# Identity products in TensorE's waits, and the product stage's buffers in another order, in a two-layer image model on one core

## The chip, the cores and the metric

The kernel runs on one core of a Trainium2 chip. The metric is the device time of one execution in microseconds (us), the median of several runs. The engines are named as in the profile: PE (TensorE, with PEld for its weight loads), DVE (VectorE), ACT (ScalarE), POOL (GpSimd) and SP (SyncE, which here only issues DMAs). SBUF is the on-chip memory that tiles live in, PSUM the one that PE writes its products to; PSUM has 8 banks of 2 KB per partition.

## What is computed

A batch of 16 images, 128 channels, 32x32 pixels (1024 tokens), goes through two layers. Layer 0 has a linear attention and then a spectral filter (a long causal convolution of the tokens with 16 filters, done by FFT in the reference); layer 1 has two 3x3 convolutions and then a mixture of 64 experts. Cut to what matters:

```python
# layer 0, attention: group norm, q/k/v, softmaxes, context, output projection
qkv = jnp.einsum('bcn,oc->bon', xf, w_qkv)
...
q = jax.nn.softmax(q, axis=-2) * SCALE
k = jax.nn.softmax(k, axis=-1)
context = jnp.einsum('bhdc,bhec->bhde', k, v)
out = jnp.einsum('bhde,bhdc->bhec', context, q)
...
# layer 0, spectral part
out = jnp.einsum('btkd,k,kde->bte', U_plus, s, Mpp)
out = out + jnp.einsum('btkd,k,kde->bte', U_minus, s, Mpm)
...
# layer 1, convolutions
out = _conv3x3(x, w1, stride=1)
out = jax.nn.relu(_bn(out, gamma1, beta1, mean1, var1))
out = _conv3x3(out, w2, stride=1)
out = _bn(out, gamma2, beta2, mean2, var2)
return jax.nn.relu(out + residual)
...
# layer 1, experts: each picks its 8 best tokens, pools them, runs two dense layers
h = jax.nn.gelu(jnp.einsum('ebd,edh->ebh', h, weight1), approximate=False)
...
out = jnp.einsum('ebh,eho->ebo', h, weight2)
...
outputs = outputs.at[jnp.arange(Bn)[:, None], flat_idx].add(weighted)
```

Each part is added to its input; everything is float32.

## The kernel before

The program runs through four stages, in this order. Between them it closes its pools of tiles (named regions of SBUF or PSUM) and opens new ones in the same memory.

**Attention** (classes and functions around L344 to L758; pools `aconst`, `setup`, `work`, `spool`, `xpool`, `ppool` in SBUF and `ps` in PSUM). One sample is a list of small steps, each a method of `Attention`; the table `period` (L729) gives for each step how many samples ahead it runs, and the loop over `p` from -6 to 15 (L747) calls all steps of a period in the order of the table. The engines PE, DVE, ACT and POOL keep the program's order. The first periods are sparse, since only the steps far ahead have a sample to work on. `tokens` transposes a sample on PE (L152), `channels` transposes it back (L162), `k` makes the keys (L439), `group` is a product of one column (L390). The entry `filters` advances a generator that prepares the filters' spectrum: its second step multiplies `phi` by `wf` on PE (L644), later ones load and combine the matrices M_phi into `mst` (L670, L675). Near its end each sample passes through the butterflies on POOL (L277 to L299) into `xf`, one tile of 1 MB in chunks of frequencies, and `odd_turns4` stores it into DRAM tensor `vd` by one DMA (L615). `taps_add` stores the sample itself into `xd` (L634). PSUM tiles carry the tag `big` (3 buffers of two banks) or `s` (2 buffers).

**Products** (L762 to L877). The spectrum has 16 chunks of frequencies. For each chunk `generate` makes a matrix `g` of 64 KB per partition on PE from `mst` and `ph` (L790, PSUM tiles `pg`), `collect` copies it to SBUF by DVE and ACT (L801, L803), `begin` loads the samples' spectra `xc` from `vd` in four batches of four samples (L778) and has POOL build `v` from each batch (L781, L782), `multiply` multiplies `v` by `g` on PE (L814) into PSUM tiles `py`. ACT copies `py` to `yt` (L875), `combine` (L842, L843) adds and subtracts its two halves on DVE, `finish` does the last butterflies on POOL, in the last chunk on DVE (L828 to L831), and stores the chunk to `yd` by two DMAs (L835). Chunk c+1 is generated while chunk c is multiplied, so there are two buffers for `g`, each in a pool of its own (`gpl0`, `gpl1`); chunk 0 uses the first, chunk 15 the second. The pools are opened in the order `gpl0`, `gpl1`, `cpl` (with `v`, `ys`, `ye`, `yt`), `xcl` (`xc`), `psg` (8 PSUM banks). `yd` has two parts: the last two chunks are in the second.

**Convolutions and routing** (L889 to L1489). Pools `cconst`, `first`, `xpool2`, `cwork` in SBUF, `cps` in PSUM (tags `big`, `cv`, `s`). A sample again is a list of steps, methods of `Routed`. Here the order is worked out by a small planner, `planned`, from a table of engine, duration, due time and dependences. `load(b)` loads the sample and its spectrum: the first sample and the first parts of `y` of samples 0 and 1 through POOL's queue, all else through SP's. Then SP loads the convolutions' weights `cw` (L1456) and small vectors. `inverse` (L1087) transforms back on PE, `tokens`, `image`, `channels` are transposes, `conv` makes the products of both convolutions (L969), `logits` (L1274) the routing scores of a pair of samples, `turn` (L152) transposes the gates, `pool` (L1321) gathers the chosen tokens, `pooled` (L1334) transposes the result.

**Experts and output** (L1493 to L1601). For each group of four experts: `hidden` (L1500, L1507), gelu on ACT (L1512), `turn` (L1520), `output` (L1531), `collect` (L1542). The weights stream through a ring of 14 buffers, which are reused buffers of the convolution stage. At the end the experts' results are transposed (L1568), combined with `ob` on DVE (L1572), multiplied by the gates (L1590), added to the samples, and stored (L1601).

A pool that is opened over memory of an earlier pool waits, in every first use of its tiles, until the earlier pools in its place are altogether released. A pool opened with `reuse_waits="tile"` waits tile by tile for those earlier tiles that lay in the same place. Before, only the last pool of the output stage does so (L1581).

Of the kernel before, what the change touches and what calls it, by code (L numbers as in the profile page):

```python
# [8 lines left out]
F32 = mybir.dt.float32  # L9
AF = mybir.ActivationFunctionType  # L10
ALU = mybir.AluOpType
# [3 lines left out]
P = 128  # L15
# [17 lines left out]
NCH = 16  # L33
# [36 lines left out]
def metaformer_kernel(ctx: ExitStack, tc: tile.TileContext, io: dict, out: bass.AP):  # L70
# [83 lines left out]
    def transpose_in_classes(pt, src):  # L154

        for q in range(NQ):
            nc.tensor.transpose(pt[:, q, :], src.rearrange("c (s q) -> c q s", q=NQ)[:, q], ident)

    def transpose_out(pt, src):

# [6 lines left out]
    with ExitStack() as l0:  # L167
# [43 lines left out]
        with ExitStack() as a0:  # L211
# [128 lines left out]

            def small(shape, name):
                return work.tile(shape, F32, name=name, tag=name, bufs=5)

            class Attention:  # L344

# [266 lines left out]

                def odd_turns4(self):
                    butterflies(self.ao, self.xf, 1, self.sd)
                    nc.sync.dma_start(  # L615
                        vd[:, :, self.b, :].rearrange("c p w -> p c w"),
                        self.xf.rearrange("p c x r m j -> p c (x r m j)"),
                    )

                def taps(self):  # L620

# [124 lines left out]
            with tc.manual_schedule(engines=PINNED):  # L746
                for p in range(-reach, B):  # L747
                    next(preparing, None)
                    for name, d in period:
                        b = p + d  # L750
                        if name == "filters":
                            next(setting, None)
                        elif 0 <= b < B:
                            if name == "tokens":
                                samples[b] = Attention(b)
                            getattr(samples[b], "q_" if name == "q" else name)()
                assert next(preparing, None) is None
                for _ in setting:  # L758
                    pass


        with ExitStack() as g0:  # L762
            gpl = [g0.enter_context(tc.tile_pool(name=f"gpl{i}", bufs=1)) for i in range(2)]
            cpl = g0.enter_context(tc.tile_pool(name="cpl", bufs=2))
            xcl = g0.enter_context(tc.tile_pool(name="xcl", bufs=1))
            psg = g0.enter_context(tc.tile_pool(name="psg", bufs=8, space=PSUM))
            gs, vs = {}, {}
            NB = EPR // 4

# [69 lines left out]

            def combine(c, m, ys, t):  # L840

                nc.vector.tensor_tensor(ys[:, :, 0, m], t[:, 1], t[:, 0], ALU.add)  # L842
                nc.vector.scalar_tensor_tensor(  # L843
                    ys[:, :, 1, m], t[:, 1], -1.0, t[:, 0], ALU.mult, ALU.add
                )
                if m == NM - 1:
                    finish(c, ys)

            with tc.manual_schedule(engines=PINNED):
# [5 lines left out]
                for c in range(NCH):  # L855
# [4 lines left out]
                    for m in range(NM):  # L860
# [10 lines left out]
                        fresh = set()  # L871
                        for x in range(2):
                            multiply(c, m, x, py, fresh)
                        t = cpl.tile([P, 2, JL // RG, C], F32, name="yt", tag="yt", bufs=1)
                        nc.scalar.copy(t, py)  # L875
                        waiting = c, m, ys, t
                combine(*waiting)  # L877


# [11 lines left out]
    with ExitStack() as c1:  # L891

        cconst = c1.enter_context(tc.tile_pool(name="cconst", bufs=1))
        first = c1.enter_context(tc.tile_pool(name="cfirst", bufs=1))
        xpool = c1.enter_context(tc.tile_pool(name="xpool2", bufs=1))
        work = c1.enter_context(tc.tile_pool(name="cwork", bufs=2))
        cps = c1.enter_context(ExitStack())
        ps = cps.enter_context(tc.tile_pool(name="cps", bufs=2, space=PSUM))

# [73 lines left out]
        def big():  # L975
            return ps.tile([P, N], F32, name="big", tag="big", bufs=2)

        def tokens(t):
            return t.rearrange("p (j c) -> p j c", c=C)

# [2 lines left out]
        def load(b):  # L983
# [3 lines left out]
            (nc.sync if b else nc.gpsimd).dma_start(xt[b], xd[b])  # L987
            yts[b] = first.tile([P, 2, 2 * NM, C], F32, name="y", tag="y", bufs=2)
            for i, js in enumerate((slice(P - 2 * JL), slice(P - 2 * JL, P))):
                (nc.gpsimd if b < 2 and i == 0 else nc.sync).dma_start(  # L990
                    yts[b][js].rearrange("p r x e -> p r (x e)"),
                    yd[i][:, :, b].rearrange("j r x e -> j r (x e)"),
                )
# [458 lines left out]
        with tc.manual_schedule(engines=PINNED | {mybir.EngineType.SP}):  # L1452
# [5 lines left out]
            for j in range(2):  # L1458
                nc.sync.dma_start(b2[j * E : (j + 1) * E, :], w2[:, HID, :])
            samples = [None] * B  # L1460
            for b, name in order:
                if name == "yin":
                    if b > 1:
# [8 lines left out]
                if name == "tokens2":  # L1472
                    if b // 2 in AWAY:
                        nc.sync.dma_start(xd[b], samples[b].x)
                    if b % 2 == 0 and b // 2 - 1 in AWAY:
                        load_half(b // 2 - 1 - AWAY[0])
                if b == B - 1 and name == "inverse":
                    for h in range(5, 9):
                        load_half(h)
# [68 lines left out]
        with tc.manual_schedule(engines=PINNED):  # L1548
# [18 lines left out]
            for q in range(NPAIR):  # L1567
                nc.tensor.transpose(  # L1568
                    pob[:, q, :], ot[:, 2 * q : 2 * q + 2, :].rearrange("p j e -> p (j e)"), ident
                )  # L1570
            for q in range(NPAIR):
                nc.vector.scalar_tensor_tensor(  # L1572
                    ob[:, q], pob[:, q], rs[:, q : q + 1], ob[:, q], ALU.mult, ALU.add
# [183 lines left out]
```

## Time and profile before

| what | us |
|---|---|
| median of 3 runs | 1266.36 |
| the runs | 1265.75, 1269.21, 1266.36 |
| the profiled execution | 1271.15 |
| its span, first to last instruction | 1269.4 |
| mean granted clock of PE | 0.965 |

Busy shares of the span: PE 91%, DVE 74%, ACT 57%, POOL 48%.

| stage | from about | to about |
|---|---|---|
| attention | 0 | 387 |
| products | 387 | 669 |
| convolutions and routing | 681 | 1166 |
| experts | 1166 | 1239 |
| output | 1239 | 1269 |

How to read it: "L814 PE MATMUL py<-g,v 128*32 128x128 f32 x8" is eight matrix instructions of line 814 that write tile `py` from `g` and `v`; a float32 product of the program is two such instructions. In the timeline the first two numbers are start and length in us, and the bracket gives how long the engine stood idle before and what the profile thinks released it. A wait for several things is put down to the one that came last in the record. "SPq" and "POOLq" are queues of an engine on which DMAs are issued; a DMA in the chain of waits is drawn from its issue to its landing. The granted clock is the share of full speed that PE was given.

### The profile page before, as it was taken

The numbers are of one execution on the slowest core, as the hardware profiler recorded it, in microseconds if no ns is written. First come the engines' busy times: TensorE is split into PE (matmuls) and PEld (weight loads), VectorE is DVE, ScalarE is ACT, GpSimd is POOL, SyncE is SP. The second block draws the span as 40 slices with busy tenths as digits, with TensorE's granted clock in tenths as the row PEclk, the third lists the DMA queues.
The fourth block names the chain that finished last, engine by engine and source line by source line (L and its number), as shares of the span: only waits on it lengthen the run. The fifth ranks groups of instructions, "written<-read, shape, count | busy, mean of one in ns | idle before, by whom it ended". The sixth has DMA issues, their size and how long they took to land. (4 is left out here: it accounts for less than half of the span.)

```text
span 1269.4 us, 34066 instructions
## 1 busy us (share of the span) xinstructions
PE 1149.6 (91%) x14244; PEld 934.4 (74%) x14244; DVE 934.9 (74%) x1944; ACT 726.0 (57%) x1420; POOL 603.9 (48%) x801
## 2 busy tenths in 40 slices
PE   4889999999997999999994999999999999986995
PEld 3677777777776988888883888888888888862442
DVE  5788888887774777776764799888898988881235
ACT  4777777767554777777761355555655655543111
POOL 2335545565566688887872434343333433220002
PEclk8999999999998999999997999999999999996998
DMA  7105343443336344444448423233233223245996
GB/s 264 33 30 165 117 138 124 133 158 92 125 118 192 94 137 136 131 133 126 124 137 268 112 51 83 83 98 120 83 100 117 72 95 113 88 147 186 353 378 265
DMA packets 91226, 175.13 MB, mean 138 GB/s; under 512 B 5952, under 2 KB 42048, under 8 KB 90432
## 3 DMA queue, kind: packets, MB, share of 16 engines
q1 hardware_dynamic: 90192, 169.54, 40.8%
q0 software_dynamic: 880, 3.41, 0.8%
q8 instruction: 112, 1.84, 0.6%
q14 instruction: 42, 0.34, 0.1%
HBM read 110.28 MB, written 62.65 MB: 136 GB/s over the span
## 5 line engine op out<-in xcount | busy, mean ns | idle before, releaser
L969 PE MATMUL pcv<-v,cw 128*128 128x256 f32 x1152 | 258.2, 380 | 1.3 <-POOL v L1157 1.3
L969 PEld LDWEIGHTS pcv<-v,cw 128*128 128x128 f32 x1152 | 214.7, 190 | 34.4 <-issue 4.9
L801 DVE COPY g<-pg 128x512 f32<-128x512 f32 x196 | 128.2, 682 | 82.4 <-PE pg L790 82.2
L803 ACT COPY g<-pg 128x512 f32<-128x512 f32 x316 | 161.4, 606 | 32.5 <-PE pg L790 31.6
L790 PE MATMUL pg<-ph,mst 32*128 32x128 f32 x4096 | 140.9, 278 | 7.4 <-issue 5.9
L790 PEld LDWEIGHTS pg<-ph,mst 32*128 32x128 f32 x4096 | 127.2, 187 | 20.7 <-issue 13.9
L814 PE MATMUL py<-g,v 128*32 128x128 f32 x4096 | 128.4, 276 | 10.5 <-POOL v L781 6.0
L814 PEld LDWEIGHTS py<-g,v 128*32 128x32 f32 x4096 | 110.2, 111 | 21.8 <-POOL v L781 6.4
L144 ACT ACTIVATE tok<-tok,sts 128x128 f32<-128x128 f32 x256 | 101.9, 480 | 16.8 <-DVE sts L1044 13.4
L135 DVE BATCH_NORM_STATS2 bst<-big 128x6 f32<-128x256 f32 x256 | 91.0, 416 | 21.5 <-PE big L152 12.4
L781 POOL TENSOR_TENSOR v<-xc 128x256 f32<-128x256 f32 x128 | 100.4, 807 | 9.3 <-DVE g L801 9.3
L626 PE MATMUL big<-u,mu 128*128 128x128 f32 (+4 forms) x384 | 86.0, 380 | 0.0
L1157 POOL TENSOR_TENSOR v<-abss 128x256 f32<-128x256 f32 x64 | 49.0, 786 | 68.1 <-DVE abss L1153 56.7
L277 POOL TENSOR_TENSOR xf<-ab 128x256 f32<-128x256 f32 x34 | 24.7, 727 | 114.0 <-DVE ab L244 113.9
L1176 POOL TENSOR_TENSOR yo<-abss 128x256 f32<-128x256 f32 x32 | 23.5, 734 | 108.9 <-DVE abss L1172 108.9
L626 PEld LDWEIGHTS big<-u,mu 128*128 128x128 f32 x384 | 56.7, 191 | 18.0 <-issue 15.4
L875 ACT COPY yt<-py 128x512 f32<-128x512 f32 x64 | 37.5, 585 | 51.7 <-PE py L814 31.3
L559 PE MATMUL big<-wf,ub 128*128 128x256 f32 x256 | 63.6, 393 | 0.2
L144 ACT ACTIVATE tt<-tt,sts 128x128 f32<-128x128 f32 x128 | 51.1, 481 | 14.6 <-DVE sts L1044 14.6
L1598 POOL TENSOR_TENSOR xb<-yt,xb 128x1024 f32<-128x1024 f32 x3 | 7.1, 2353 | 107.6 <-ACT yt L1597 107.6
L782 POOL TENSOR_SCALAR v<-v 128x256 f32<-128x256 f32 x64 | 55.0, 860 | 5.6
L464 POOL TENSOR_TENSOR ke<-ke,ks 128x1024 f32<-128x1024 f32 x16 | 30.6, 1913 | 55.7 <-DVE qs L472 44.1
(251 smaller groups left out, 2493.7 us busy)
## 6 DMA issues: line engine op xcount, KB each, us to landing
we<-in_weight SPq DMA_DIRECT2D x32, 1024.0 KB, 7.9
vd<-xf SPq DMA_DIRECT2D x16, 1024.0 KB, 5.1
xc<-vd SPq DMA_DIRECT2D x64, 256.0 KB, 3.4
yd<-ys SPq DMA_DIRECT2D x32, 512.0 KB, 3.8
y<-yd SPq DMA_DIRECT2D x14, 896.0 KB, 6.6
x<-in_x SPq DMA_DIRECT2D x16, 512.0 KB, 4.4
mi<-in_M_phi SPq DMA_DIRECT2D x16, 512.0 KB, 4.6
xd<-x SPq DMA_DIRECT2D x16, 512.0 KB, 6.1
```

The costliest lines, as they stand in the source:

```text
L135: nc.vector.bn_stats(bst[:, j : j + 2, :].rearrange("p j s -> p (j s)"), src[:, j : j + 2, :].rearrange("p j c -> p c j"),)
L144: nc.scalar.activation(dst[:, j, :], src[:, j, :], AF.Identity, bias=nm[:, j : j + 1], scale=r[:, j : j + 1],)
L559: nc.tensor.matmul(dst, self.ub[:, q, :], wf[:, q, :], start=True, stop=True)
L626: nc.tensor.matmul(self.pa[:, a:hi], mu[:, NF - 1 - si, tap, :], self.u[:, a - tap : hi - tap], start=(tap == 0), stop=(tap == KU - 1),)
L781: nc.gpsimd.tensor_tensor(vv[:, x, 1:, bs], e, o, op)
L782: nc.gpsimd.tensor_scalar(v[:, :, 0, bs], v[:, :, 2, bs], -1.0, None, ALU.mult)
L790: nc.tensor.matmul(pg[r][:, i], mst[rs, 4 * q + i, :], ph[rs, c, :], start=True, stop=True,)
L801: nc.vector.tensor_copy(dst, src)
L803: nc.scalar.copy(dst, src)
L814: nc.tensor.matmul(py[rows, x, kl, :], v[:, (x * NM + m) * JL + jl, 1 - ri : 3 - ri, :] .rearrange("p k b -> p (k b)"), g[:, ((x * 2 + ri) ...
L969: nc.tensor.matmul(pc[:, i], wt[:, dy, k, :], v[:, k, dy * WT : dy * WT + HT], start=(dy == 0), stop=(dy == 2),)
L1157: nc.gpsimd.tensor_tensor(v[:, k, WT : WT + HT], self.ab[:, 0], self.ab[:, 1], op)
```

## The change

It has these parts.

1. A helper `keep` writes `count` products of the identity with itself (128x256, one product each) into a PSUM tile `wm` that nobody reads. It takes a buffer of tag `s` in attention and of tag `cv` later. It is called in attention after `tokens` of sample 1 (9 products), after the first `filters` entry after the first period (8), after `channels` of sample 0 (3) and `k` of sample 1 (3); at the head of the convolution stage (26); after `turn` (4) and `pooled` (8) of sample 13, `logits` (11) and `turn` (1) of sample 15; and before the last combination with `ob` (4).
2. The store of the last sample's spectrum to `vd` is split: chunk 0 alone, then chunks 1 to 15.
3. In the product stage the pools are opened in the order `gpl0`, `cpl`, `gpl1`, `xcl`, `psg`, and all but `gpl0` wait tile by tile.
4. In the last chunk ACT copies only the first half of `py`, into one of two slots of `yt`, and DVE reads the second half from PSUM.
5. The pools of the convolution stage except `cconst` wait tile by tile.
6. The first part of `y` of sample 1 is loaded through SP's queue, not POOL's.

```diff
+    def keep(ps, tag, count):
+
+        if count:
+            wm = ps.tile([P, 2, P], F32, name="wm", tag=tag, bufs={"s": 2, "cv": 3}[tag])
+        for _ in range(count):
+            nc.tensor.matmul(
+                wm, ident, ident.unsqueeze(1).to_broadcast([P, 2, P]), start=True, stop=True
+            )
...
+            idle = {("tokens", 1): 9, ("filters", 0): 8, ("channels", 0): 3, ("k", 1): 3}
...
-                    nc.sync.dma_start(
-                        vd[:, :, self.b, :].rearrange("c p w -> p c w"),
-                        self.xf.rearrange("p c x r m j -> p c (x r m j)"),
-                    )
+                    for cs in (slice(0, 1), slice(1, NCH)) if self.b + 1 == B else (slice(NCH),):
+                        nc.sync.dma_start(
+                            vd[cs, :, self.b, :].rearrange("c p w -> p c w"),
+                            self.xf[:, cs].rearrange("p c x r m j -> p c (x r m j)"),
+                        )
...
                         if name == "filters":
                             next(setting, None)
+                            keep(ps, "s", idle.pop((name, 0), 0) if p > -reach else 0)
...
                             getattr(samples[b], "q_" if name == "q" else name)()
+                            keep(ps, "s", idle.get((name, b), 0))
...
-            gpl = [g0.enter_context(tc.tile_pool(name=f"gpl{i}", bufs=1)) for i in range(2)]
-            cpl = g0.enter_context(tc.tile_pool(name="cpl", bufs=2))
-            xcl = g0.enter_context(tc.tile_pool(name="xcl", bufs=1))
-            psg = g0.enter_context(tc.tile_pool(name="psg", bufs=8, space=PSUM))
+            gpl = [g0.enter_context(tc.tile_pool(name="gpl0", bufs=1))]
+            cpl = g0.enter_context(tc.tile_pool(name="cpl", bufs=2, reuse_waits="tile"))
+            gpl.append(g0.enter_context(tc.tile_pool(name="gpl1", bufs=1, reuse_waits="tile")))
+            xcl = g0.enter_context(tc.tile_pool(name="xcl", bufs=1, reuse_waits="tile"))
+            psg = g0.enter_context(tc.tile_pool(name="psg", bufs=8, space=PSUM, reuse_waits="tile"))
...
-                nc.vector.tensor_tensor(ys[:, :, 0, m], t[:, 1], t[:, 0], ALU.add)
-                nc.vector.scalar_tensor_tensor(
-                    ys[:, :, 1, m], t[:, 1], -1.0, t[:, 0], ALU.mult, ALU.add
-                )
+                a, b = t
+                nc.vector.tensor_tensor(ys[:, :, 0, m], b, a, ALU.add)
+                nc.vector.scalar_tensor_tensor(ys[:, :, 1, m], b, -1.0, a, ALU.mult, ALU.add)
...
-                        t = cpl.tile([P, 2, JL // RG, C], F32, name="yt", tag="yt", bufs=1)
-                        nc.scalar.copy(t, py)
-                        waiting = c, m, ys, t
+                        if c + 1 < NCH or m == 0:
+                            t = cpl.tile([P, 2, JL // RG, C], F32, name="yt", tag="yt", bufs=1)
+                        if c + 1 < NCH:
+                            nc.scalar.copy(t, py)
+                            waiting = c, m, ys, (t[:, 0], t[:, 1])
+                        else:
+                            nc.scalar.copy(t[:, m % 2], py[:, 0])
+                            waiting = c, m, ys, (t[:, m % 2], py[:, 1])
...
-        first = c1.enter_context(tc.tile_pool(name="cfirst", bufs=1))
-        xpool = c1.enter_context(tc.tile_pool(name="xpool2", bufs=1))
-        work = c1.enter_context(tc.tile_pool(name="cwork", bufs=2))
+        first = c1.enter_context(tc.tile_pool(name="cfirst", bufs=1, reuse_waits="tile"))
+        xpool = c1.enter_context(tc.tile_pool(name="xpool2", bufs=1, reuse_waits="tile"))
+        work = c1.enter_context(tc.tile_pool(name="cwork", bufs=2, reuse_waits="tile"))
...
-        ps = cps.enter_context(tc.tile_pool(name="cps", bufs=2, space=PSUM))
+        ps = cps.enter_context(tc.tile_pool(name="cps", bufs=2, space=PSUM, reuse_waits="tile"))
...
+        idle = {(13, "turn"): 4, (13, "pooled"): 8, (15, "logits"): 11, (15, "turn"): 1}
...
-                (nc.gpsimd if b < 2 and i == 0 else nc.sync).dma_start(
+                (nc.gpsimd if b + i == 0 else nc.sync).dma_start(
...
             samples = [None] * B
+            keep(ps, "cv", 26)
...
+                keep(ps, "cv", idle.get((b, name), 0))
...
+            keep(ps, "cv", 4)
             for q in range(NPAIR):
                 nc.vector.scalar_tensor_tensor(
```

## The prediction

> **What bounds the kernel now.** I read the clock row of the page first, then what PE waited for, then the timeline where the long waits lie, then the chain of waits.
>
> Page, slices of 31.7 us (tenths):
>
> ```profile
> PE   4889999999997999999994999999999999986995
> PEclk8999999999998999999997999999999999996998
> ```
>
> PE is the bound almost everywhere. The slices that miss are the start, slice 12 (attention to products), slice 21 (products to convolutions), and slices 35-36 and 39 (end of the convolutions, output). In four of these five the granted clock is low too.
>
> PE's waits (total, times, longest):
>
> ```profile
> PE big L1087 <- DMA y<-yd: 16.2, 1, 16.2
> ...
> PE big L152 <- DVE rs L1301: 7.1, 7, 5.5
> ...
> PE py L814 <- POOL v L781: 6.0, 1, 6.0
> PE big L644 <- DMA phi<-in_phi: 6.0, 1, 6.0
> ...
> PE pfy L1590 <- DVE ob L1572: 2.3, 1, 2.3
> ```
>
> Each is one event at one of those places, so a change there is worth its own wait plus the slow clock after it.
>
> Busy time in stretches (length, busy PE, PEld, DVE, ACT, POOL, clock, DMA share, GB/s):
>
> ```profile
> 400.00:410.00 10.00, 3.16 (x56) 2.53 (x60) 1.03 (x2) 1.05 (x3) 9.64 (x14) 0.59 0.41 110
> ...
> 670.00:680.00 10.00, 0.00 (x0) 0.00 (x0) 0.00 (x0) 0.00 (x0) 0.00 (x0) 0.50 0.81 266
> 680.00:690.00 10.00, 6.10 (x37) 5.75 (x38) 6.22 (x11) 0.00 (x0) 5.25 (x7) 0.75 0.92 310
> ```
>
> The clock halves after a gap and DMA, not PE, fills 670-690. Timeline of the first boundary:
>
> ```profile
> 388.88 0.37 SPq L615 DMA_DIRECT2D vd<-xf  x1
> ...
> 389.35 4.25 SPq L634 DMA_DIRECT2D xd<-x  x1
> ...
> 398.12 1.42 POOL L781 TENSOR_TENSOR v<-xc 128x256 f32<-128x256 f32 x2 [9.27 <-DVE g L801]
> ...
> 405.87 0.66 PE L814 MATMUL py<-g,v 128*32 128x128 f32 x8 [6.00 <-POOL v L781]
> ```
>
> POOL sits idle 9.27 us; the DVE named was working all along, so the true releaser is another: the store of xd, issued at 389.35, lands 8.5 us later, 397.85. Chain of waits, second boundary and tail:
>
> ```profile
> 669.62 8.89 DMA yd<-ys
> ...
> 686.34 14.09 DMA y<-yd
> ...
> 1148.09 4.77 PE big L1274 x8
> ...
> 1161.43 3.73 PE pp L1321 x32
> 1166.45 1.94 PE ph L1500 x8
> ...
> 1202.99 1.00 PE ph L1500 x8
> ```
>
> The same L1500 group takes 1.94 us early and 1.00 later: the tail runs at half clock until 1180.
>
> **What the skill says.** "TensorE: Matmul & The Clock Gate", Part 1: the clock is judged in free-running windows of 3413 ns, half rate after an idle one. The trace agrees: its clock steps (12.65, 19.45, 26.3, 401.8, 412.0, 668.0, 685.1, 1145.9, 1180.0, 1241.5) lie on a 3.413 us grid within 0.06. On that grid, windows with PE busy up to 0.34 all lost the clock, two of 0.43 kept it, one of 0.44 and one of 0.52 lost it; regaining took a window of 0.92 or more, and some of 0.98 to 1.00 did not do. The same page, Part 4: transposes don't count as busy the same way; the trace has one stretch made of them (1144.9-1148.0) and it lost the clock. "DMA: Bandwidth & Descriptors", Queues, rings and completion order: each ring is consumed in order; the trace agrees, y waits 14.09 us behind 2.3 MB of cw. No page bears on the pools' waits.
>
> **Price of one identity product.** 128x256 f32, two instructions. L969 has the shape: x12 in 2.59 us, 0.216 each, so 0.43 us a call at full clock, 0.86 at half.
>
> **A. Start (keep 9, 8, 3, 3).** PE ends the second token transposes at 10.1 and waits for phi until 16.1. Nine calls fill 10.1-14.0 (their PSUM slot is free at 9.5). The L644 group then took 5.35 us for 16, ending 21.45; warm it is 16 x 0.216 = 3.46: 1.9 less. DVE sat idle 5.12 us on it (through ACT's L235), so this moves everything. Eight calls end at 23.0, before L390 (25.8 - 1.9 = 23.9); then L152 1.73 becomes 1.04 and L162 1.91 becomes 1.07, partly beside ACT. Bounds 0 (a window with 0.4 of activity ends the clock anyway) to 3.4; I take 2.0. The threes lie in waits of 2.0-2.1 us (before 31.48 and 46.97): nothing.
>
> **B. Attention to products.** Summing the tiles in the order of the pools (KiB per partition): attention's work tiles lie at 51-147, xf at 147-163, the x tiles at 163-195. Before, the matrix buffers take 26-154 and v lies at 154 and up, over xf and x, hence the wait for xd's landing. After, the product buffers lie at 90-134, over work tiles only, whose last reader is POOL's L299 at 388.85. So POOL starts when the first xc lands, 387.4 + 3.3 = about 390.7, and does three batches of 2.3 us (1.42 + 0.85) by 397.6. The fourth needs the last sample's vd store; its chunk 0 now goes alone and first, so that xc no longer waits for the whole 1 MB at 396.6 but only for SP to come past xd at 393.6. It queues behind vd and xd, which leave the engines by 396: landed about 397, v whole at 399.9. PE ends its generation of g at 399.87, held by the copies into g (DVE 389.00 to 398.66). The 6.00 and 0.97 us of stalls go, and with them the half clock of 401.8-412.0: the second py group, at 413.26 before, comes one period of 3.88 us after 399.87, at 403.75, 9.5 earlier. The new late one is g's copies, level with v. The second matrix buffer now lies over xf and x and waits for 397.85, but it is first written at about 399.2. psg by tile lets PE begin 1.4 us sooner, but g's copies start at 388.9 all the same: 0.1. If the fourth xc lands 2-3 us later, 6.5 remains. I take 9.0.
>
> **C. Products to convolutions.** Chunk 14 reads the first matrix buffer for the last time near 656.4; xp0 and y0 lie over it alone. By tile, POOL's load of x0 no longer waits for the last product (3.40 us of idle, 666.21) but goes after L831 at 662.8; y0 follows. y1's first part leaves POOL's queue and stands on SP behind y0's second part. The last chunk's half copies take ACT from 0.59 to about 0.35: 0.25. Before the yd store's landing DMA then has 3.5 MB, not 4.4, and 3.4 us more: landed near 673.6, not 678.5. PE's first inverse moves from 681.87 to about 677.5; 26 calls from 665.6 end at 665.6 + 11.2 = 676.8, just before. But SP now has y1's 0.9 MB ahead of cw, x2, y2: 3.3 us at 280 GB/s. y2, which lands at 700.43 and gates DVE's L1016 and so the first conv a, gains only 4.9 - 3.3 = 1.6; the path through sample 0 gains 4.4. Both meet at conv a. I take 2.8; bounds 0 and 4.4. Memsets and the other tiles' waits are hidden by those loads.
>
> **D. Tail (keep 4, 8, 11, 1).** Fours fill the 2.33 us before L1321 (1134.93), which is warm then, 1.97 not 3.06, but DVE's L1232 ends at 1139.25 in any case: 0.2. Eight (3.45) lie in the 4.35 us gap before 1144.92. The transposes there are paced by ACT (8 x 0.38); a window mostly of them may lose the clock all the same. If not, logits end at about 1150.9, not 1152.84: 2.0, taken at half, 1.0. Eleven (4.7) lie in 5.55 us. L152 1.94 to 1.06: 0.9. L1321 3.68 to 1.97: 1.7. From its end, before: L1500 for group 2 ends 15.3 us later (1180.37). After: ACT's L1552 (2.44) and table load (1.28) hold the first gelu until 3.9; then 0.6, L1520 0.75, L1500 and L1507 2.13, L1531 1.08, 0.75, 1.07: 10.2. Gain 5.1. Later groups run at 3.94 us as before: weights queue ahead by over 10 us (14 halves landed by 1148). Sum 0.2 + 1.0 + 0.9 + 1.7 + 5.0 = 8.8; bounds 2 and 10.
>
> **E. Output (keep 4).** 1.7 us in the 2.33 before 1240.88. The first four pairs fall from 3.4 to 1.7; the first store goes 1.6 earlier, and stores of 8 MB near 400 GB/s then set the end: 1.5.
>
> **Sum.** 2.0 + 9.0 + 2.8 + 8.8 + 1.5 = 24.1. PE is the bound between these places, so they add. The profiled execution took 1271.15 (span 1269.4 and 1.75 around): it would be 1247. It lies 4.8 above the median of 1266.36, which is what I forecast from: 1242.
>
> **Rivals.** (1) The calls don't bridge all gaps (windows at 0.4 of activity): A 0, D 3, E 0.5, B and C as above less a little: 14, so 1252. For it: windows of 0.44 and 0.52 that lost the clock. Against: two of 0.43 that kept it, and the calls fill most gaps to 0.8. (2) Everything carries: A 3.4, B 9.5, C 4.4, D 10, E 1.6: 29, so 1237. Against it is y2's place on SP. (3) Slower: the identity products themselves run at half clock, 0.86 a call, and stand before the work they precede. Eight at the start end 2.5 late; 26 end near 685.7, 3.8 after the old first inverse; eight and eleven push L152 to 1163.5, 5.1 late; the last four 1.1. That is 12.5 lost against B's 9.0: 1270. It decides from about 0.76 us a call. Against it: L969 in the same shape holds full clock all through the convolutions. (4) The tile waits do nothing: B stands by the new order of pools alone, C is lost: inside the range.
>
> **Chances.** Forecast 0.53 (own range 1237-1248), (1) 0.22, (2) 0.18, (3) 0.05, (4) 0.02. Leaving out (3) and the outer ends of (1) and (2): 1233 to 1255. About 0.3%, 4 us, is what can be told from no change: faster 0.93, same 0.02, slower 0.05.
>
> **What would show it.** B: POOL's first v near 391, no PE wait at py, clock 1.0 in that slice. C: xp0 issued near 663, inverse near 4 us earlier, y2's landing against it. D: L1274, L1321 and the first L1500 at 2-3, 2.0 and 1.0 us. E: first store 1.5 us sooner after the last transposes. I am wrong if the clock row still falls at these places, or if a keep group ends after the wait it lies in.

## The result, and the profile after

| | before | after |
|---|---|---|
| median | 1266.89 (1266.36 in the first three) | 1252.55 |
| single runs | 1265.75 to 1269.21 | 1249.26 to 1255.48 (4 runs) |
| the profiled execution | 1271.15 | 1249.26 |
| its span | 1269.4 | 1247.5 |
| mean granted clock in it | 0.965 | 0.994 |

The ratio is 0.9884, 95% interval 0.9851 to 0.9917: 14.3 us faster by the medians, 21.9 us between the two profiled executions. The forecast was 24.1 us, to 1242. The time lies inside the outer range given (1233 to 1255), outside the forecast's own (1237 to 1248); the gain is 10 us short of the forecast. The profiled execution of the changed kernel is the shortest of its four, that of the kernel before lies above all its runs shown: the difference between 21.9 and 14.3 is part of the answer.

Line numbers have moved: L644 is now L656, L781 L796, L814 L829, L790 L805, L969 L988, L1274 L1295, L1321 L1342, L1500 L1523, L1590 L1614; the identity products are L164. One identity product is called a call below, as in the prediction. First the two rows of the page, slices of 31.2 us:

```profile
PE   7889999999999999999988899999999999998996
PEclk9999999999999999999999999999999999999998
```

Slice 0 rises from 4 to 7, slice 12 from 7 to 9, slice 36 from 6 to 8. Slices 20 to 22, the second boundary, show 8s where one slice showed 4. The start, in the timeline of before and of after:

```profile
16.10 5.35 PE L644 MATMUL big<-wf,phi 128*128 128x256 f32 x16 [6.00 <-DMA phi<-in_phi]
```

```profile
10.53 4.19 PE L164 MATMUL wm<-ident 128*128 128x256 f32 x18
15.88 3.69 PE L656 MATMUL big<-wf,phi 128*128 128x256 f32 x16 [1.16 <-DMA phi<-in_phi]
```

PE's waits after (total, times, longest):

```profile
PE pg L805 <- issue: 8.2, 16, 1.1
...
PE pcv L988 <- POOL v L1178: 2.7, 1, 2.7
...
PE py L829 <- issue: 2.3, 1, 2.3
...
PE big L152 <- DVE rs L1322: 1.9, 7, 0.6
```

The waits of 16.2, 6.0 and 6.0 us are gone or down to 1.2 us (the first is filled by the identity products, which can't be told from work here), but one ahead of the convolutions' products (before: L969 after POOL's L1157) has grown from 1.3 to 2.7 us, and waits that nothing releases ("issue") have grown from 5.9 + 2.0 to 8.2 + 2.3 us. Timeline of the first boundary:

```profile
385.39 3.95 SPq L646 DMA_DIRECT2D xd<-x  x1
386.80 1.43 POOL L796 TENSOR_TENSOR v<-xc 128x256 f32<-128x256 f32 x2 [2.33 <-PE pg L805]
...
394.77 1.42 POOL L796 TENSOR_TENSOR v<-xc 128x256 f32<-128x256 f32 x2 [0.94 <-DMA xc<-vd]
...
395.56 0.43 PE L829 MATMUL py<-g,v 128*32 128x128 f32 x8 [0.18 <-POOL v L796]
```

POOL begins 1.4 us after SP starts on xd's store, and no longer 8.8 after; PE's first product waits 0.18 us, not 6.00. The chain of waits (start, length), second boundary and tail:

```profile
660.44 5.13 DMA yd<-ys
...
675.28 13.68 DMA y<-yd
693.53 7.09 PE pcv L988 x24
...
1137.92 3.82 PE big L1295 x8
...
1149.45 2.02 PE pp L1342 x32
```

The store of yd takes 5.13 us, not 8.89. The 24 products of L988 take 7.09 us: the records show the clock at half from 693.48 to 696.89, after the wait of 2.72 us ahead of them. The logits took 4.77 and now 3.82, L1342 3.73 and now 2.02.

### The profile page after: what moved, and what is told of

The parts are those of the page before. It is cut to its first block, busy times and chain, and to the rows that moved or that the text cites. A ratio compares the mean times of both kernels' runs of the same rounds, so it can differ in the third digit from the quotient of the medians.

```text
span 1247.5 us, 34359 instructions
## 1 busy us (share of the span) xinstructions
PE 1166.0 (93%) x14398; PEld 952.3 (76%) x14398; DVE 940.9 (75%) x1944; ACT 725.2 (58%) x1420; POOL 603.1 (48%) x800
## 3 DMA queue, kind: packets, MB, share of 16 engines
q1 hardware_dynamic: 90448, 170.46, 41.2%
## 4 chain that ended last, share of the span: by engine, by line
PE 60%; DVE 23%; ACT 7%; DMA 4%; issue 4%; POOL 2%; SPq 0%; POOLq 0%; ACTq 0%; DVEq 0%
PE pg L805 10%; PE pcv L988 10%; PE py L829 10%; PE big L638 6%; DVE bst L135 4%; PE big L152 3%; PE big L171 3%; PE big L570 2%; PE big L450 2%; PE big L533 2%; PE big L432 2%; DMA y<-yd 2%; DVE abss L1231 1%; DVE xp L1253 1%; ACT tt L144 1%
## 5 line engine op out<-in xcount | busy, mean ns | idle before, releaser
L988 PE MATMUL pcv<-v,cw 128*128 128x256 f32 x1152 | 259.9, 382 | 2.7 <-POOL v L1178 2.7
L988 PEld LDWEIGHTS pcv<-v,cw 128*128 128x128 f32 x1152 | 215.9, 191 | 36.3 <-issue 4.9
L805 PE MATMUL pg<-ph,mst 32*128 32x128 f32 x4096 | 144.2, 280 | 9.2 <-issue 8.2
L805 PEld LDWEIGHTS pg<-ph,mst 32*128 32x128 f32 x4096 | 128.7, 186 | 25.7 <-issue 16.7
L829 PE MATMUL py<-g,v 128*32 128x128 f32 x4096 | 125.1, 274 | 4.6 <-issue 2.3
L829 PEld LDWEIGHTS py<-g,v 128*32 128x32 f32 x4096 | 108.2, 110 | 12.7 <-POOL v L797 2.6
L796 POOL TENSOR_TENSOR v<-xc 128x256 f32<-128x256 f32 x128 | 99.0, 797 | 3.3 <-PE pg L805 2.3
L286 POOL TENSOR_TENSOR xf<-ab 128x256 f32<-128x256 f32 x34 | 24.8, 729 | 110.4 <-DVE ab L253 110.3
L144 ACT ACTIVATE tt<-tt,sts 128x128 f32<-128x128 f32 x128 | 51.1, 481 | 14.5 <-DVE sts L1065 14.5
L570 PEld LDWEIGHTS big<-wf,ub 128*128 128x128 f32 x256 | 46.2, 190 | 8.8 <-ACT xn L423 3.0
```

Source lines behind the costliest of these rows:

```text
L144: nc.scalar.activation(dst[:, j, :], src[:, j, :], AF.Identity, bias=nm[:, j : j + 1], scale=r[:, j : j + 1],)
L570: nc.tensor.matmul(dst, self.ub[:, q, :], wf[:, q, :], start=True, stop=True)
L796: nc.gpsimd.tensor_tensor(vv[:, x, 1:, bs], e, o, op)
L805: nc.tensor.matmul(pg[r][:, i], mst[rs, 4 * q + i, :], ph[rs, c, :], start=True, stop=True,)
L829: nc.tensor.matmul(py[rows, x, kl, :], v[:, (x * NM + m) * JL + jl, 1 - ri : 3 - ri, :] .rearrange("p k b -> p (k b)"), g[:, ((x * 2 + ri) ...
L988: nc.tensor.matmul(pc[:, i], wt[:, dy, k, :], v[:, k, dy * WT : dy * WT + HT], start=(dy == 0), stop=(dy == 2),)
```

## Experiments

Each kernel's time stands against runs of the kernel before that were taken beside it on the same chip: the first four experiments on one chip, all others on another. To see where time went, I cut each profile at the same instructions: the end of the last attention product (L626 before), the 65th product instruction of the product stage (the 413.26 of the prediction), the stage's last, the convolutions' 25th, their last, the end of the experts' last transposes (L1568). In us; in brackets PE's idle time over 0.3 us that nothing releases. The convolutions took 422.7 to 423.7 in all and are left out.

| kernel | attention ends | first products | products (unreleased) | to convolution 25 | tail | output | span |
|---|---|---|---|---|---|---|---|
| before | 386.3 | 26.9 | 252.4 (7.8) | 42.1 | 107.5 | 30.8 | 1269.4 |
| after | 382.0 | 18.9 | 255.8 (9.7) | 41.2 | 98.7 | 27.9 | 1247.5 |
| a1_after | 385.2 | 18.5 | 257.7 (12.7) | 43.5 | 99.0 | 27.9 | 1254.9 |
| a2_keeps_only | 382.6 | 26.9 | 255.3 (10.0) | 44.3 | 98.5 | 28.1 | 1259.4 |
| a3_pools_only | 386.5 | 18.8 | 247.7 (4.7) | 45.0 | 101.2 | 30.8 | 1253.2 |
| a4_order_alone | 388.9 | 19.1 | 248.0 (4.2) | 48.3 | 102.2 | 31.5 | 1261.3 |
| b1_shift41 | 388.8 | 20.7 | 249.7 (6.2) | 42.6 | 98.8 | 29.3 | 1253.0 |
| b2_shift9 | 385.2 | 23.2 | 250.3 (5.7) | 41.0 | 98.2 | 28.0 | 1249.0 |
| b3_shift25 | 386.2 | 19.7 | 240.7 (1.3) | 44.4 | 98.9 | 28.0 | 1240.9 |
| b4_y2_first | 382.3 | 20.8 | 253.2 (8.9) | 40.0 | 98.6 | 28.0 | 1245.9 |
| c1_wide64 | 383.8 | 19.6 | 250.2 (7.2) | 41.6 | 100.8 | 28.0 | 1247.1 |
| c2_wide64_y2 | 382.7 | 18.8 | 241.7 (2.4) | 40.4 | 98.8 | 28.0 | 1233.3 |
| c3_y1_on_pool | 382.0 | 19.8 | 255.8 (11.4) | 42.5 | 100.8 | 28.0 | 1251.6 |
| c4_keep_transposes | 384.4 | 19.1 | 259.6 (13.0) | 40.1 | 101.1 | 27.1 | 1254.5 |

### The change in parts

The kernel before, beside these four: 1263.19 (51 runs, all but one between 1257.15 and 1273.49). The profiled 1271.15 lies far up in this spread. Its mean granted clock was 0.965; the middle one of the 50 is 0.9685. The changed kernel once more:

> The changed kernel again, for the spread of its times. Theory P (the median is 14 below before, not 24, because the grid of clock windows falls differently in each execution and a drop or two stays in most of them): times spread over 1248 to 1256, and the mean clock of an execution goes with its time, 0.990 for the long and 0.994 for the short. Theory Q (the first profile was an odd one and the change is worth 14): times within 1251 to 1254, and the profile shows the stage gains to be smaller than in the first one at the same clock.

Measured: 1248.65, ratio 0.9886 (0.9842 to 0.9929). The gain by medians is 14.5 us again; the 21.9 between the first two profiles doesn't hold. Its six runs spread from 1245.11 to 1257.13, and the two longest have the lowest clocks (0.988 and 0.989, the others 0.992 to 0.994): theory P rather than Q.

The identity products alone, with the old pools and loads:

```diff
+                            keep(ps, "s", idle.get((name, b), 0))
...
+            keep(ps, "cv", 26)
...
+                keep(ps, "cv", idle.get((b, name), 0))
...
+            keep(ps, "cv", 4)
```

> The kernel before with the identity products alone: old pools, old order, old queues. If the steps add up: start 2 to 4, nothing at the first boundary (POOL still begins its v near 398 less the start's gain, PE still waits 6 us), nothing at the second, tail near 9, output 1.5 to 3, so 1251 to 1254. Rival (the products hold the clock only where the loads of the new pools also come earlier, or are mostly luck): less than 6 gained, above 1260. In the profile L1321 of the last pair takes 2.0 and L1500 of the first group 1.07 in the first case.

Measured: 1261.35, ratio 0.9977 (0.9961 to 0.9993). The number is the rival's, but the pieces that it doubted are there: attention ends some 4 us sooner (382.0 to 385.2 with calls in the three profiles so far, 386.3 to 388.9 in the three without), the last L1321 takes 1.97 us and not 3.68, the output is some 3 us shorter. The product stage (2.9 us longer than before) and the second boundary (2.2) give 5 us back.

The buffers alone (all but the identity products):

```diff
+        count = 0
         if count:
```

> The changed kernel with no identity product (the counts are 0); pools, split store, queues and half copies stay. If the steps add up: first boundary 8 to 9, second 1 to 3, so 1255 to 1258; the clock still falls at 12.6, near 668 and four times after 1130. Rival (the product stage gives part back to waits for instructions, 3.5 us in the first profile): 1259 to 1261, and the product stage from its second py group to its last is 255 to 256 us long and not 252.4.

Measured: 1257.15, ratio 0.9949 (0.9931 to 0.9968). The number is inside the 1255 to 1258, but not as the sum had it: the first boundary gained 8.1 us as expected, while the second lost 2.9 in the profile where 1 to 3 were to be gained. PE's first inverse comes 13.0 us after the last product there and no longer 16.2, but y of sample 2 lands 36.2 us after it (before: 34.8). Only the new order of the product stage's pools, and the split store, with the old waits:

```diff
-            gpl = [g0.enter_context(tc.tile_pool(name=f"gpl{i}", bufs=1)) for i in range(2)]
+            gpl = [g0.enter_context(tc.tile_pool(name="gpl0", bufs=1))]
             cpl = g0.enter_context(tc.tile_pool(name="cpl", bufs=2))
+            gpl.append(g0.enter_context(tc.tile_pool(name="gpl1", bufs=1)))
...
+                    for cs in (slice(0, 1), slice(1, NCH)) if self.b + 1 == B else (slice(NCH),):
```

> The kernel before with only the new order of the product stage's pools and the split store; every pool still waits for whole pools. Theory O (the place of the buffers is what counts: the work tiles under them are free at 388.9): POOL's first v near 391, PE's wait at py below 2 us, 1257 to 1259. Rival W (the tile waits do it): POOL's first v near 398 as before, the 6 us wait stays, 1265 to 1267.

Measured: 1263.86, ratio 1.0004 (0.9972 to 1.0035). Its timeline at both boundaries:

```profile
392.27 3.74 SPq L635 DMA_DIRECT2D xd<-x  x1
393.33 1.42 POOL L783 TENSOR_TENSOR v<-xc 128x256 f32<-128x256 f32 x2 [1.98 <-ACT g L805]
...
402.61 0.43 PE L816 MATMUL py<-g,v 128*32 128x128 f32 x8 [0.22 <-POOL v L783]
```

```profile
665.18 0.62 POOL L989 DMA_DIRECT2D xp<-xd  x1 [10.70 <-DMA yd<-ys]
...
679.29 2.04 PE L1089 MATMUL big<-wi,y 128*128 128x128 f32 x8 [23.38 <-DMA y<-yd]
```

At the first boundary the order does everything: 26.9 us become 19.1 here and 18.8 with tile waits, and the identity products do nothing there (26.9). At the second it is given back: x and y of sample 0 start on POOL's queue at 665.18, when the last store of yd has landed, 9.3 us after the last product (before: 0.6), and land with SP's loads at 679.20. The wait is 23.38 us instead of 16.2. With tile waits that load starts 3.8 us ahead of the last product (a3), so the tile waits keep part of what the order gains; half copies and the other queue for y of sample 1 also differ between the two kernels and were not taken apart here. Theory O was right about POOL and PE, and its 1257 to 1259 wrong: it had not looked at the second boundary.

The tails of the last two kernels are that of the kernel before, instruction for instruction on PE. Yet they take 101.2 and 102.2 us, not 107.5. The first two groups of L1500, in stretches (length, busy PE, PEld, DVE, ACT, POOL, clock, DMA share, GB/s), of before, of order alone, of buffers alone:

```profile
1166.45:1178.68 12.23, 11.51 (x73) 3.65 (x73) 0.98 (x2) 3.71 (x8) 0.00 (x0) 0.50 0.74 252
```

```profile
1162.98:1170.52 7.54, 6.41 (x72) 2.55 (x72) 0.98 (x2) 3.71 (x8) 0.00 (x0) 1.00 0.85 302
```

```profile
1155.39:1163.08 7.69, 6.41 (x73) 2.55 (x73) 0.98 (x2) 3.85 (x8) 0.00 (x0) 1.00 0.87 296
```

After has 7.69 there as well. In both these kernels, which have no identity products, the clock comes back before this stretch; in the profile of before it stayed at half until 1180. What that stretch gained between the two first profiles, 4.5 us, doesn't need the calls. (With them, two of ten further profiles took 10.4 us there, after a fall of the clock at 1153 and 1158: they don't settle it either.) No second profile of the kernel before shows how often it stays at half so long.

### Instruction blocks in the product stage

In the product stage PE, which is busy almost all the time, stands still now and then, and nothing releases it. Of the changed kernel, timeline:

```profile
507.36 1.61 PE L805 MATMUL pg<-ph,mst 32*128 32x128 f32 x46 [0.88 <-issue]
...
512.18 1.06 PE L805 MATMUL pg<-ph,mst 32*128 32x128 f32 x28 [0.47 <-issue]
```

and the page's rows of DMA queues:

```profile
q8 instruction: 113, 1.85, 0.6%
```

113 packets of 16.4 KB for 28,982 recorded PE instructions: 256 to a packet. Counting PE's recorded instructions from the start, of 163 unreleased waits over 0.35 us (weight loads, product stage of the table, all 14 profiles) 160 fall on number 193 or 194 of a block of 256. In the changed kernel ten of the eleven of PE's over 0.4 us in that stage end 2.2 to 2.4 us after a q8 packet has started. The two above: packets at 505.01 and 509.76, PE goes on at 507.36 and 512.18. So these are waits for instructions. The Trainium skill, "Runtime: NRT & Kernel Launch", section Instruction fetch mechanics, states blocks of 16 KiB, 256 instructions, and calls the crossing "mostly hidden". The block's size agrees; the cost doesn't: here a crossing costs up to 2.3 us, and the waits of the stage add up to 9.7 us.

A chunk of the stage makes 1024 PE instructions, four blocks, so a boundary falls on the same place of the loop in every chunk. The 23 identity products before the stage are 92 instructions and move it. To move it further I put narrow products of the identity at PE's head, 41, 9 and 25 of them in three kernels:

```diff
+            ws = ps.tile([P, 2, P], F32, name="ws", tag="s")
+            for _ in range(41):
+                nc.tensor.matmul(ws[0:32, 0], ident[:, 0:32], ident, start=True, stop=True)
             for n in range(2):
                 pw = ps.tile([P, P], F32, name="pw", tag="s")
```

> The changed kernel with 41 more, narrow products (32 columns of the identity into an unread tile, about 31 ns an instruction pair, some 3 us in all) in TensorE's first wait, from 2.5 to 5.9 us. They add 41 x 4 = 164 PE instructions ahead of the product stage, which with the 92 of the identity products there make 256. Theory F (instruction fetch): in the product stage PE's idle stretches without a releaser all end 2.2 to 2.4 us after the start of a 16 KB packet of the instruction queue, and fall on number 193 or 194 of a block of 256 instructions; the identity products moved the blocks against the loop, from a place that costs 251.5 us (pools alone, order alone) to one that costs 259.5 to 261.3. Back at a whole block the stage takes 250 to 253 us, such waits sum to 5 to 7 us and not 14 to 16, and the time is 0.6% below the changed kernel's: ratio to before about 0.982. Theory R (the waits are chance, or come from the DMA load): stage 258 to 262 us, ratio 0.9886 as before.

> The same with 9 narrow products, 36 instructions, so that the blocks stand half a block (128) from where they stood before the change. F: the stage's length differs from that of the changed kernel (259.5 to 261.3 us) by more than its two profiles differ from each other, in the direction that the place in the loop gives; its level can't be told ahead. R: 258 to 262 us, ratio 0.9886.

> The same with 25 narrow products, 100 instructions, three quarters of a block (192). F and R as for half a block: F wants the stage's length to change with the place, R wants 258 to 262 us in all three.

Measured against 1263.06: 1252.97, ratio 0.991 (0.9888 to 0.9932); 1244.71, 0.9864 (0.9828 to 0.9901); 1242.70, 0.9866 (0.9819 to 0.9914). By the place in the block, with all kernels of the table:

| PE instructions added ahead, modulo 256 | product stage | unreleased |
|---|---|---|
| 0 (before, a3, a4, b1) | 247.7 to 252.4 | 4.2 to 7.8 |
| 92 (after, a1, a2, b4, c3, c4) | 253.2 to 259.6 | 8.9 to 13.0 |
| 128 (b2) | 250.3 | 5.7 |
| 192 (b3, c1, c2) | 240.7 to 250.2 | 1.3 to 7.2 |

The expectations count the stage from the ninth product instruction, 3.4 to 6.4 us more than the table. In that count b1, b2 and b3 took 254.9, 256.7 and 244.3 us: all below theory R's 258 to 262, b1 above F's 250 to 253. The six at 92 lie above all eight others, whatever their pools: theory F holds for that step. Among the other places the spread at one place is too wide to rank them. By the whole time none of the three ratios is told from the changed kernel's 0.9884, since the intervals overlap. My price for the narrow products was wrong. They took 11.93 us for 41:

```profile
2.54 11.93 PE L347 MATMUL ws<-ident 128*32 128x128 f32 x82 [2.54 <-POOL ident masks.py:199]
```

That is 0.145 us for a matrix instruction with its weight load where I had taken 31 ns, attention ended at 388.8, and b1's total missed its 0.982.

Next, the same shift without that cost: 64 columns and twice the calls where the change has 256.

```diff
-                wm, ident, ident.unsqueeze(1).to_broadcast([P, 2, P]), start=True, stop=True
+                wm if tag == "cv" else wm[:, 0, 0:64],
+                ident,
+                ident.unsqueeze(1).to_broadcast([P, 2, P]) if tag == "cv" else ident[:, 0:64],
+                start=True, stop=True,
...
-            idle = {("tokens", 1): 9, ("filters", 0): 8, ("channels", 0): 3, ("k", 1): 3}
+            idle = {("tokens", 1): 19, ("filters", 0): 17, ("channels", 0): 6, ("k", 1): 6}
```

> The changed kernel with the 23 identity products of the attention stage (128x256) replaced by 48 products of 128x64 (19, 17, 6 and 6 in the same places). 48 x 4 = 192 instructions stand then ahead of the product stage, the place in the block at which 25 narrow products gave a stage of 244.3 us, without their cost at the head (PE busy with them until 10.8 us). Theory F: product stage 243 to 247 us and not 258 to 261, waits without a releaser 3 to 5 us; attention ends as in the changed kernel (382 to 385 us), if 64 columns keep the clock as 256 do: about 1234 us, ratio 0.977. Rival: 64-column products don't keep the clock, or take longer than their gaps: attention ends at 386 to 389, ratio 0.980. If the short stage of 244 us was chance: ratio 0.9886.

Measured: 1244.98 against 1266.56, ratio 0.9841 (0.9807 to 0.9875), short of the 0.977. Attention ends at 383.8, so the 64 columns did what the 256 did; but the profile has a stage of 250.2 us with 7.2 us of such waits, though it stands at the same place as b3 with 240.7 and c2 with 241.7. The place shifts the cost; it doesn't fix it. What else decides when a packet is asked for stays open.

### The second boundary

```diff
-            for n in range(2):
-                nc.sync.dma_start(cw[n], cwd[n])
+            nc.sync.dma_start(cw[0], cwd[0])
...
                     if b > 1:
                         load(b)
+                    if b == 2:
+                        nc.sync.dma_start(cw[1], cwd[1])
```

> The changed kernel with the second half of the convolutions' weights (cw1) loaded after sample 2's x and y, not before. Theory Y: at the second boundary y of sample 2 sets the first convolution's second part; it lands at 688.96 in the changed kernel, behind cw1 (1.15 MB, about 4 us at 280 GB/s). Without that ahead of it it lands near 685, the wait of 2.72 us before the second part goes, and with it the clock's fall at 693.5 (1.6 us): conv stage's 24th product 3 to 4.5 us earlier after the last product of the stage before, ratio about 0.985. Rival: the first convolution waits for POOL and DVE in any case (four z steps of 0.9 us each), or cw1 now comes too late for the second convolution: within 1 us, ratio 0.9886.

Measured: 1248.43, ratio 0.9884 (0.9845 to 0.9922). The wait of 2.72 us is gone, y of sample 2 lands 21.5 us after yd and not 23.4 (a1: 24.8), and the boundary takes 40.0 us, not 41.2 and 43.5, less than the 3 to 4.5 us expected. The chain above has PE wait for y of sample 2. But counted from the last product it lands after 32.2 us here, where the changed kernel had 32.3 and 36.3, so how much of the gain is its doing isn't shown. The time shows no gain: 1 to 3 us are less than these intervals can tell. The same with 64-column products:

> The same with the second half of the convolutions' weights loaded after sample 2's y. By its trace that took 1 to 3 us out of the second boundary, by its time nothing. If the gain is there: 1 to 2 us below the kernel without it in this call, ratio 0.975; rival: equal within 1 us.

Measured: 1239.46 (1235.12 to 1241.90), ratio 0.9798 (0.9765 to 0.9831): 5.5 us below c1, more than either expectation. In the profiles the boundary accounts for 1.2 (41.6 to 40.4), while the product stages, whose code is the same, lie 8.5 us apart; what makes up the rest of the 5.5 isn't shown. It is the fastest kernel here, and its interval lies below that of the changed kernel. PE's row and the clock's:

```profile
PE   6889999999999999999998999999999999998996
PEclk9999999999999999999998999999999999999998
```

Then y's first part of sample 1 back on POOL's queue:

```diff
-                (nc.gpsimd if b + i == 0 else nc.sync).dma_start(
+                (nc.gpsimd if b < 2 and i == 0 else nc.sync).dma_start(
```

> The changed kernel with y's first part of sample 1 back on POOL's queue. The prediction held that on SP's queue it costs y of sample 2 3.3 us (0.9 MB at 280 GB/s). Theory P: off SP's queue, y of sample 2 lands 20 us after the last landing of yd and not 23.4 (changed kernel), and the convolutions' 24th product comes 2 to 3 us sooner after the last product of the stage before (changed kernel: 41.2 and 43.5 us in two profiles); ratio about 0.986. Rival: the same bytes pass the same engines, and POOL's queue is the slower one (y of sample 0 takes 9.9 us on it): y of samples 1 and 2 land no sooner, 41 to 45 us, ratio 0.9886 or above.

Measured: 1253.70, ratio 0.9907 (0.9878 to 0.9936). Chain of waits:

```profile
661.39 8.81 DMA yd<-ys
...
678.11 14.76 DMA y<-yd
```

The store of yd takes 8.81 us, as in the kernel before (8.89), where the changed kernel had 5.13 and, in a1, 7.70; that the load on POOL's queue competes with it fits, but one profile isn't proof. y of sample 2 lands 35.2 us after the last product, against 32.3 and 36.3 in the two profiles of the changed kernel. The move costs y of sample 2 nothing that can be seen; the rival holds.

### Transposes for products

```diff
-            nc.tensor.matmul(
-                wm, ident, ident.unsqueeze(1).to_broadcast([P, 2, P]), start=True, stop=True
-            )
+            for h in range(2):
+                nc.tensor.transpose(wm[:, h], ident, ident)
```

> The changed kernel with each identity product replaced by two 128x128 transposes of the identity. Theory T: the clock's windows don't count transposes; the calls keep nothing. The clock falls near 12.6 and 26 us, and in the last third as without calls: stretch from the last convolution to the experts' last transposes 101 to 107 us and not 98.3 to 99.0, output 31 us and not 28; ratio 0.993 to 0.996. Rival: they count: tail 98.3 to 99.0, output 28, ratio 0.9886 or somewhat less, since two transposes take about 0.26 us and a product 0.43.

Measured: 1258.87, ratio 0.9939 (0.9911 to 0.9967). The clock falls at 16.6 and 26.8 us and twice in the tail, where after has one fall: as theory T has it, and the ratio too. The tail's 101.1 us decide nothing, since c1 and c3 with products took 100.8. Output is 27.1 and not 31, which T doesn't have. Its first calls, timeline:

```profile
10.20 2.13 PE L165 MATMUL wm<-ident 128*128 128x128 f32 x18
16.31 5.38 PE L655 MATMUL big<-wf,phi 128*128 128x256 f32 x16 [3.98 <-DMA phi<-in_phi]
```

Nine calls end after 2.13 us, and PE then idles 3.98; the nine products took 4.19 and left 1.16. The run can't tell "not counted" from "too short": with 3.98 us of idle behind transposes the next group takes 5.38 us as before the change (5.35), with 1.16 us behind products 3.69.

## Why the prediction was right in direction and too high in size

Between the two first profiles the parts add up to the whole: attention 4.4, first products 8.0, product stage -3.4, second boundary 0.9, convolutions 0.3, tail 8.8, output 2.9: 21.9. By step:

- **A, 2.0.** The group L644 fell from 5.35 to 3.69, 1.7 for the 1.9, and the first keys came 2.45 us sooner. Attention ended 4.4 sooner. The further 1.9 are two falls of the clock, at 70.7 and 278.9, that this profile lacks; a1 has both, and its attention ends 1.1 us sooner than before. The calls don't decide them.
- **B, 9.0.** Measured 8.0. POOL's first v came at 386.80, with 4.4 us of A at 391.2 for "about 391". The missing 1.0 is the fourth batch: its v at 394.77, with 0.18 and 1.20 us of waits left at PE where I had none. That the order of the pools alone carries B was right (a4), and so that far was rival (4). That without the tile waits C would merely be lost was wrong: with whole-pool waits C turns 6.2 us worse.
- **C, 2.8.** Measured 0.9 in the first profile, minus 1.4 in a1. The load of x0 was issued 5.2 us before the last product (a1: 1.9), for the 2.8 that I had, and yd landed 8.9 us after it (a1: 11.4), for 12.9 before and 8.0 forecast. y of sample 2 landed 2.5 us sooner after the last product than before, for the 1.6 that I had, but 1.5 later in a1. Two terms failed. y of sample 1 on SP was to cost y of sample 2 3.3 us; c3 shows no such price. And I stopped at y2's landing: PE's wait behind it grew from 1.30 to 2.72 us, and the products then run at half clock until 696.89, 1.6 us, where before they ran at full.
- **D, 8.8.** Measured 8.8 by the two profiles, with L1274 0.9, L152 0.9, L1321 1.7, and the stretch from L1321 to L1500 of group 2 down from 15.25 to 9.95, 5.3 for the 5.0. To hit 8.8 was luck: a3 and a4, with no call, take 9.95 us for that stretch too, and by their tails the calls are worth 101.7 - 98.8 = 2.9. **The step that failed is "L1500 for group 2 ends 15.3 us later"**: I took the half clock until 1180, one execution's, for the kernel's, and subtracted its repair from the median, which holds less of it or none. Setting 24.1 against 1266.36 after having noted that the profile lies 4.8 above it was the inconsistency. What is the calls' own is L1321: 1.97 us in all ten profiles with products, 3.68 in the three without. My reading of the transposes was off as well: the fall at 1145.87 follows a window (1142.46 to 1145.87) in which PE was busy 0.24, before most of them ran. In the changed kernel a window all but filled by transposes (1133.80 to 1137.21, PE busy 0.64) did lose the clock, as I had allowed for, and L1274 gained 0.9 of a possible 2.0.
- **E, 1.5.** Measured 2.9: PE's products begin 1.8 us after the transposes, not 2.3, DVE's first add 2.0 after that, not 3.3, and the rest is 1.1 us shorter. Why that last part is, stays open; nine of eleven profiles with calls show 27.9 to 28.1, the three without 30.8 to 31.5.
- **"PE is the bound between these places, so they add."** This is the second step that failed. The product stage got 3.4 us longer (5.3 in a1), because, by the table of places, the identity products moved the instruction blocks; against the other kernels at place 0 (247.7 to 249.7) it is 6 to 10.
- **Rival (3)**, calls at half clock: nine took 4.19 us, 0.47 a call, eight 0.45; full clock. The 26 ended within 0.1 us of the first inverse.
- **Rival (1)**, calls that don't bridge the gaps, said 1252, and 1252.55 was measured. That is chance: its 0 for A and 0.5 for E came out as 4.4 and 2.9, and the clock row has no low slice where the calls stand. Its 3 for D is what a3 and a4 leave.
- **Two smaller readings.** The clock was low in all five places that I named, not in four. And "windows with PE busy up to 0.34 all lost the clock" leaves out the first 5.8 us, in which PE stood still and no fall is on record.

With A without its two falls at 2.5, B at 8.0, C at -1.4 to 0.9, D at 2.9, E at 2.9 and the product stage at -5.3 to -3.4, the parts come to 9.6 to 13.8 us, near the 14.3 and 14.5 of the medians but below them. Single profiles don't allow more, since they scatter, and the parts don't add: the two halves of the change, identity products alone and buffers alone, gain 1.8 and 6.0 us by their medians, together 7.9 and not 14.5. Part of that is the second boundary, where each half alone takes longer than before (44.3 and 45.0 against 42.1) and both together 41.2 and 43.5.

## What to carry to other kernels

A stretch at a low clock in one profile may be that execution's alone: before pricing its repair, ask for the time of an average run, or look at the same stretch in a second profile. Instructions that cost nothing where they stand still move everything behind them in the instruction stream; where PE issues short instructions in a long loop, look for waits without a releaser at a fixed distance of instructions. And a boundary between stages has two sides: a new order of buffers that frees the first may hold up the second, so look at both; waits tile by tile gave a part of it back here.

## What the runs showed of the hardware

- PE's instructions arrive in packets of 256 (113 packets for 28,982), and a wait for one was up to 2.3 us long. Over all kernels here the waits without a releaser cost 1.3 to 13.0 us of a product stage of about 250, by the place of the block boundary and by something that remains unknown.
- One kernel's runs on one chip differ by 16 us (1257.15 to 1273.49, 50 runs), and the profiles show why in part: falls of the clock near 70 and 279 us come and go between executions of the same code.
- A matrix instruction of 32 columns on the identity took 0.145 us at the program's head; in the product stage one of the same shape (L829, 64 in 1.96 us) takes 31 ns. The 41 products all write the same 32 partitions, those of L829 go round four groups of 32; whether that is the difference was not tried.
